# Moving the scan's input from PSUM into the scan's own result tile in SBUF

## The chip, the cores and the metric

The kernel runs on one core of one Trainium2 chip. The metric is the device time of one execution in microseconds (us). All verdicts below compare fast runs of kernels on the same chip; the profiles that are compared can be of different chips. "Before" is the kernel without the change, "after" the kernel with it.

## The reference, cut to what matters

The program is a network of four layers. The change touches layer 0 alone, a selective scan over 4096 pixels for 4 images, 4 directions, 192 channels and 16 states:

```python
def step(h, inp):
    d_t, u_t, b_t, c_t = inp
    dA = jnp.exp(d_t[..., None] * A)
    h = dA * h + (d_t * u_t)[..., None] * b_t[:, :, None, :]
    y = jnp.einsum('bkdn,bkn->bkd', h, c_t)
    return (h, y)
```

The other layers (a deformable convolution with gathers, a Fourier layer, feed-forward layers, attention) run beside the scan on the same engines, image by image.

## The kernel before

The scan is cut into 1536 units of 128 partitions (8 channels x 16 states) by 1024 pixels. Five engines hand each unit on, and the emission loop keeps the stages some units apart:

```python
# Layer0.scan: the stages of iteration n, in order (cut)
(self.inflow, n + 1), (self.total, n - 3 if n % 2 else -1), (self.decay, n + 2),
(self.keep, n - 1), (self.recur, n), (self.weigh, n - 1)

def decay(self, u):                      # ACT: da = exp(A * delta), in SBUF (five tiles)
    ...
    self.net.nc.scalar.activation(u.da, u.da, AF.Exp, scale=self.al[:, a : a + 1])

def inflow(self, u):                     # PE: db = delta * u, spread to 128 partitions
    db = self.ps.tile([128, 2, CH], F32, name=f"db{u.key}", tag="db", bufs=2)   # PSUM
    ...                                  # two matmuls, one for each half

def recur(self, u):                      # VectorE
    nc = self.net.nc
    nc.vector.tensor_mul(u.db, u.db, u.bc[:, 0, :])                              # L741
    u.hh = self.sp.tile([128, T], F32, name=f"hh{u.key}", tag="hh", bufs=3)      # SBUF
    first = 0.0 if u.step == 0 else u.state[:, u.n : u.n + 1]
    nc.vector.tensor_tensor_scan(                                                # L744
        u.along(u.hh), u.along(u.da), u.along(u.db), first, ALU.mult, ALU.add
    )

def keep(self, u):                       # ACT: the last column of hh is the next state
    ...
def weigh(self, u):                      # GpSimd: hc = hh * C
    u.hc = self.sp.tile([128, T], F32, name=f"hc{u.key}", tag="hc", bufs=3)
    self.net.nc.gpsimd.tensor_mul(u.hc, u.hh, u.bc[:, 1, :])                     # L755
def total(self, u, v):                   # PE: sums hc over the states (L772)
    ...
```

In PSUM the kernel keeps two db tiles (2 x 512 columns each), three tiles of 512 columns for the other matmuls and one for the sums.

## Time and profile before

| | before |
|---|---|
| time, median of the runs beside the kernel after | 10,588.9 us (10,575.5 to 10,604.1) |
| profiled execution shown in the prediction | 10,460.6 us, granted clock 0.702 |
| profiled execution taken later (`e5_before_again`) | 10,584.6 us, granted clock 0.696 |

The first profile is of an execution that was 1.2% faster than the timed runs. The second one, of the unchanged kernel, is the better partner for the kernel after, and the comparisons below use it. Its busy time in the stretch of the scans and in the stretch after the last scan (columns: the stretch, its length, then PE, weight loads, VectorE (DVE), ACT, GpSimd (POOL) with their counts, TensorE's granted clock, the DMA engines' share, GB/s):

```profile
322.00:9012.00 8690.00, 5842.08 (x22116) 1795.46 (x22118) 7215.60 (x4567) 3794.76 (x5988) 5960.76 (x3199) 0.69 0.67 171
9012.00:10584.00 1572.00, 1125.13 (x6192) 640.71 (x6190) 397.17 (x367) 412.84 (x787) 446.13 (x376) 0.68 0.23 64
```

The units occupy 8690 us, 5.66 us a unit, with VectorE busy for 83% and GpSimd for 69% of that. Neither is full, so what counts is how the two interlock. Its VectorE and GpSimd groups that matter (output<-inputs, shape, count, then busy us and mean ns, then idle time before the group and what ended it):

```profile
L744 DVE TENSOR_TENSOR_SCAN hh<-da,st,db 128x1024 f32<-128x1024 f32 x1152 | 2703.7, 2347 | 170.4 <-ACT st L751 31.8 <-ACT da L725 7.5 <-POOL hc L755 2.7
L741 DVE TENSOR_TENSOR db<-db,bc 128x1024 f32<-128x1024 f32 x1536 | 1871.6, 1218 | 572.9 <-PE db L730 571.5 <-DMA da<-de 1.1
L744 DVE TENSOR_TENSOR_SCAN hh<-da,db 128x1024 f32<-128x1024 f32 x384 | 878.1, 2287 | 109.1 <-ACT st L751 34.8 <-ACT da L725 31.2 <-DVE db L741 1.9
```

```profile
L755 POOL TENSOR_TENSOR hc<-hh,bc 128x1024 f32<-128x1024 f32 x1536 | 3876.9, 2525 | 1935.5 <-DVE hh L744 990.8 <-PE py L772 775.7 <-issue 68.3
L1074 POOL DMA_INDIRECT g<-table,idx x1152 | 1435.5, 1246 | 518.1 <-issue 193.1 <-DVE s L1091 146.3 <-DVE d L1234 117.6
```

### The profile page before, as it was taken

What the parts mean: (1) busy time and instruction counts of PE and PEld (TensorE: products, weight loads), DVE (VectorE), ACT (ScalarE), POOL (GpSimd) and SP (SyncE); (2) the same over time, 40 slices, a digit from 0 to 9 for tenths busy, and PEclk for the clock granted to TensorE, in tenths of its full rate; (3) what the DMA queues carried; (4) which work ended last, traced back from release to release, by engine and by line L of the source; (5) the groups of instructions that cost most, each with busy time, mean ns of one, the idle gap of its engine ahead of it and who ended that gap; (6) DMA issues with size and microseconds to landing.
All of it is one profiled execution on the core that took longest, in us unless ns stands there. A gap on an engine that the chain in (4) does not pass through costs nothing. (4 is left out here: it accounts for less than half of the span.)

```text
span 10460.6 us, 85850 instructions
## 1 busy us (share of the span) xinstructions
PE 7119.7 (68%) x28728; PEld 2481.0 (24%) x28728; DVE 7640.0 (73%) x4993; ACT 4352.7 (42%) x6950; POOL 6456.3 (62%) x3603
## 2 busy tenths in 40 slices
PE   7565865976794555558876665678676646877686
PEld 2010200311120111113332221133322112453262
DVE  0788688587759999987878889788888897444211
ACT  4564655665454443223433433333343423313223
POOL 0675476377537888875557878655678885366301
PEclk9555855866696666667777766677677666886695
DMA  1666565566656677776677667776767676543110
GB/s 45 166 174 157 149 173 162 140 172 168 156 134 171 184 188 185 189 181 161 177 184 184 169 160 190 172 179 166 186 174 176 174 188 151 118 137 92 52 45 6
DMA packets 775576, 1605.19 MB, mean 153 GB/s; under 512 B 249305, under 2 KB 339477, under 8 KB 773022
## 3 DMA queue, kind: packets, MB, share of 16 engines
q10 hardware_dynamic: 300672, 985.79, 37.4%
q1 hardware_dynamic: 400734, 387.34, 13.8%
q0 software_dynamic: 73728, 226.57, 8.3%
q8 instruction: 228, 3.74, 0.2%
q14 instruction: 214, 1.75, 0.1%
HBM read 1343.08 MB, written 256.29 MB: 153 GB/s over the span
## 5 line engine op out<-in xcount | busy, mean ns | idle before, releaser
L755 POOL TENSOR_TENSOR hc<-hh,bc 128x1024 f32<-128x1024 f32 x1536 | 3885.8, 2531 | 1937.3 <-DVE hh L744 1003.6
L725 ACT ACTIVATE da<-da,w_al 128x1024 f32<-128x1024 f32 x1536 | 1762.6, 1149 | 3126.4 <-DMA da<-de 981.5
L730 PE MATMUL db<-du,rep 96*128 96x512 bf16 x3072 | 1293.0, 515 | 2324.6 <-DVE hh L744 2147.1
L744 DVE TENSOR_TENSOR_SCAN hh<-da,st,db 128x1024 f32<-128x1024 f32 x1152 | 2703.5, 2347 | 165.4 <-ACT st L751 28.3
L741 DVE TENSOR_TENSOR db<-db,bc 128x1024 f32<-128x1024 f32 x1536 | 1871.0, 1218 | 585.3 <-PE db L730 585.0
L1074 POOL DMA_INDIRECT g<-table,idx x1152 | 1449.7, 1258 | 417.2 <-issue 191.1
L772 PE MATMUL py<-hc,w_fold 128*32 128x512 f32 x6144 | 1303.4, 886 | 25.4 <-POOL hc L755 8.8
L730 PEld LDWEIGHTS <-rep 96*128 96x128 bf16 x3072 | 231.2, 108 | 3539.8 <-DVE hh L744 2935.0
L744 DVE TENSOR_TENSOR_SCAN hh<-da,db 128x1024 f32<-128x1024 f32 x384 | 878.0, 2286 | 104.9 <-ACT st L751 31.5
L1085 DVE TENSOR_TENSOR g<-g,wt 128x3456 f32<-128x3456 f32 x128 | 593.1, 4634 | 148.6 <-DMA g<-table,idx 147.3
L605 POOL TENSOR_TENSOR w<-w,ex 128x512 f32<-128x512 f32 x192 | 259.0, 1349 | 650.7 <-ACT w L601 648.9
L518 PE MATMUL pc<-pad,wc 96*128 96x512 f32 x1152 | 533.1, 615 | 9.1 <-DMA wc<-wc_d 6.1
L607 DVE TENSOR_TENSOR rl<-rl,w 128x512 f32<-128x512 f32 x192 | 304.9, 1588 | 95.6 <-POOL w L605 95.3
L1102 PE MATMUL ps<-w_ident,s 128*96 128x128 f32 x1152 | 265.3, 378 | 136.9 <-DVE s L1091 120.7
L1332 POOL CAST xqf<-fl 96x512 fp8e5<-96x512 f32 x64 | 51.5, 810 | 496.6 <-DVE fl L1291 496.5
L604 DVE SCALAR_TENSOR_TENSOR rl<-pd,lw 128x512 f32<-128x512 f32 x192 | 130.7, 681 | 309.6 <-ACT lw L599 309.5
L592 PE MATMUL pd<-xd,dtw 7*128 7x512 f32 (+1 forms) x512 | 324.5, 953 | 43.9 <-ACT xd L570 28.5
L1103 ACT COPY st<-ps 96x384 f32<-96x384 f32 x384 | 177.5, 474 | 419.7 <-PE ps L1102 418.2
L772 PEld LDWEIGHTS py<-hc,w_fold 128*32 128x32 f32 x6144 | 184.8, 134 | 666.0 <-issue 516.2
L1109 PE MATMUL pd<-st,wdc 96*96 96x256 f32 x1152 | 309.0, 414 | 0.0
L518 PEld LDWEIGHTS pc<-pad,wc 96*128 96x128 f32 x1152 | 220.5, 195 | 310.5 <-issue 290.4
L628 DVE TENSOR_TENSOR du<-ex,du 128x512 bf16<-128x512 f32 x192 | 234.6, 1222 | 79.7 <-ACT du L626 75.3
(241 smaller groups left out, 10039.6 us busy)
## 6 DMA issues: line engine op xcount, KB each, us to landing
da<-de ACTq DMA_DIRECT2D x1536, 512.0 KB
du<-du ACTq DMA_DIRECT2D x384, 192.0 KB
bc<-bcd ACTq DMA_DIRECT2D x128, 512.0 KB
du<-du SPq DMA_DIRECT2D x128, 384.0 KB
y<-yb SPq DMA_DIRECT2D x384, 128.0 KB
de<-rl SPq DMA_DIRECT2D x128, 256.0 KB
m<-in_dft SPq DMA_DIRECT2D x128, 256.0 KB
du<-du SPq DMA_DIRECT2D x128, 192.0 KB
```

Of the source, the lines that this page charges most:

```text
L518: nc.tensor.matmul(pp, lhsT=wc[:, q, g * 128 : (g + 1) * 128], rhs=pad[:, r0 + dy : r0 + dy + NR, dx : dx + W], start=(q == 0), stop=(q == 8),
L592: nc.tensor.matmul(o, lhsT=dtw[2 * NS :, 2 * pr + q, m], rhs=xdbl[pr, j, q][2 * NS :], start=True, stop=True)
L607: nc.vector.tensor_sub(rl, rl, w1)
L725: self.net.nc.scalar.activation(u.da, u.da, AF.Exp, scale=self.al[:, a : a + 1])
L730: self.net.nc.tensor.matmul(db[:, h, :], lhsT=self.rep[:96, u.s % 4, :], rhs=u.du[u.s // 4][:, h * CH : (h + 1) * CH], start=True, stop=True,)
L741: nc.vector.tensor_mul(u.db, u.db, u.bc[:, 0, :])
L744: nc.vector.tensor_tensor_scan(u.along(u.hh), u.along(u.da), u.along(u.db), first, ALU.mult, ALU.add)
L755: self.net.nc.gpsimd.tensor_mul(u.hc, u.hh, u.bc[:, 1, :])
L772: nc.tensor.matmul(py[p0 : p0 + 32], lhsT=self.fold[:, u.i, :], rhs=hc[:, h * CH : (h + 1) * CH], start=u.add is None and u.i == 0, stop=( ...
L1074: nc.gpsimd.indirect_dma_start(out=g[:, k, :], out_offset=None, in_=self.tables[b % 2], in_offset=bass.IndirectOffsetOnAxis(ap=idx[:, 9 * ...
L1085: nc.vector.tensor_mul(g4, g4, w4.unsqueeze(2).to_broadcast([128, 36, C]))
L1109: nc.tensor.matmul(po, lhsT=wdc[:, k, :], rhs=st[:, k, :], start=(k == 0), stop=(k == 8))
```

## The change

The intent is to give a db tile back to PE one scan earlier, as PE stands for more than 2100 us waiting for one. The product of delta u and B goes into hh, and the scan runs over hh in place:

```diff
     def recur(self, u):
         nc = self.net.nc
-        nc.vector.tensor_mul(u.db, u.db, u.bc[:, 0, :])
         u.hh = self.sp.tile([128, T], F32, name=f"hh{u.key}", tag="hh", bufs=3)
+        nc.vector.tensor_mul(u.hh, u.db, u.bc[:, 0, :])
         first = 0.0 if u.step == 0 else u.state[:, u.n : u.n + 1]
         nc.vector.tensor_tensor_scan(
-            u.along(u.hh), u.along(u.da), u.along(u.db), first, ALU.mult, ALU.add
+            u.along(u.hh), u.along(u.da), u.along(u.hh), first, ALU.mult, ALU.add
         )
```

## The prediction

> **What bounds the kernel now.** I read the page first, then the busy time by stage, then the groups of instructions, then the list of who waited for whom, then a few microseconds of the timeline. The page says that no engine is full: VectorE (DVE) is busy for 73% of the span, PE 68%, GpSimd (POOL) 62%. The groups that the change touches, each line giving output<-inputs, shape, count, then busy us and mean ns, then idle time before the group and its releasers:
>
> ```profile
> L755 POOL TENSOR_TENSOR hc<-hh,bc 128x1024 f32<-128x1024 f32 x1536 | 3885.8, 2531 | 1937.3 <-DVE hh L744 1003.6 <-PE py L772 780.0 <-issue 65.6
> L744 DVE TENSOR_TENSOR_SCAN hh<-da,st,db 128x1024 f32<-128x1024 f32 x1152 | 2703.5, 2347 | 165.4 <-ACT st L751 28.3 <-ACT da L725 7.0 <-DVE db L741 1.5
> L741 DVE TENSOR_TENSOR db<-db,bc 128x1024 f32<-128x1024 f32 x1536 | 1871.0, 1218 | 585.3 <-PE db L730 585.0
> L1074 POOL DMA_INDIRECT g<-table,idx x1152 | 1449.7, 1258 | 417.2 <-issue 191.1 <-DVE d L1234 117.6 <-DVE s L1091 42.7
> L744 DVE TENSOR_TENSOR_SCAN hh<-da,db 128x1024 f32<-128x1024 f32 x384 | 878.0, 2286 | 104.9 <-ACT st L751 31.5 <-ACT da L725 30.6 <-DVE db L741 1.4
> ...
> L1085 DVE TENSOR_TENSOR g<-g,wt 128x3456 f32<-128x3456 f32 x128 | 593.1, 4634 | 148.6 <-DMA g<-table,idx 147.3 <-issue 1.2
> ```
>
> One unit of the scan is: PE spreads delta u into a PSUM tile db, VectorE multiplies it by B (L741) and scans it (L744), GpSimd multiplies the result by C (L755), PE sums that. There are 1536 units. The first scan starts at 323 us and the last ends at 8999 us: 8676 us, 5.65 us a unit. The busy time of that stretch:
>
> ```profile
> 323.00:8999.00 8676.00, 5834.19 (x22116) 1796.32 (x22118) 7201.01 (x4567) 3794.64 (x5989) 5955.84 (x3199) 0.69 0.67 171
> ```
>
> The columns are PE, weight loads, DVE, ACT, POOL: DVE 83%, POOL 69%. So VectorE leads, with GpSimd working beside it. From the waits, the one the change is aimed at:
>
> ```profile
> PE db L730 <- DVE hh L744: 2147.1, 730, 20.4
> ...
> DVE db L741 <- PE db L730: 585.0, 179, 22.0
> ```
>
> PE[...] stands 2147 us until a scan gives a db tile back (there are two); VectorE in turn stands 585 us for the next db.
>
> The 1461 us outside the stretch hold none of these units, and I take them as unchanged.
>
> [...] Two stretches of the timeline (start us, duration us):
>
> ```profile
> 4016.10 2.29 DVE L744 TENSOR_TENSOR_SCAN hh<-da,db 128x1024 f32<-128x1024 f32 x1
> 4017.03 2.36 POOL L755 TENSOR_TENSOR hc<-hh,bc 128x1024 f32<-128x1024 f32 x1
> ```
>
> ```profile
> 4024.81 2.35 POOL L755 TENSOR_TENSOR hc<-hh,bc 128x1024 f32<-128x1024 f32 x1
> ...
> 4025.16 3.66 DVE L607 TENSOR_TENSOR rl<-rl,w 128x512 f32<-128x512 f32 x1
> ...
> 4027.11 1.16 POOL L624 TENSOR_TENSOR ex<-ex,du 128x512 f32<-128x512 f32 x1
> ```
>
> The scan, with one input in PSUM, takes its shortest 2.29 us with GpSimd's product over it. L607, with both inputs in SBUF, takes 0.67 us when GpSimd is idle; here it takes 3.66 us and ends 0.55 us after GpSimd's second instruction: it waited through both. Over all 1536 scans with the state operand or without, the durations lie within 2.285 to 2.362 us, whatever GpSimd does.
> [...] L604 (one PSUM input, 128x512) has a mean of 0.681 us, L607 undisturbed 0.665 to 0.694. [...]
> [...]
>
> **The change part by part.** The order of instructions on each engine is the same in both kernels (compared). Nothing is added or removed; two operands move.
> - L741 writes hh in SBUF in place of db in PSUM. It still has one SBUF input, so 1536 x 1.22 us stay as they are and stay free beside GpSimd. hh is taken one instruction sooner; with three buffers it was last read three units earlier. Cost 0.
> - db is free after the product, one scan (2.33 us) sooner. Most of the 2147 us of PE's standing and of VectorE's 585 us can go. PE is not the leading engine, so the gain is at most those 585 us.
> - The scan now reads da and hh, both in SBUF. [...] 3582 us of scans no longer run beside GpSimd. Taking both engines' records together, GpSimd's tensor instructions lie over scans for 1930 us today, its gathers (L1074) for another 460 us. That parallel time is lost.
>
> The work that must now take turns, within the stretch, at undisturbed durations: scans 3582; L755 1536 x 2.35 = 3610; GpSimd's small products L605, L624, L610 and L616 (192 x 1.26, 192 x 1.15, 192 x 1.27) = 707 and L835 and L879 (128 x 1.25) = 160; VectorE's other instructions with two SBUF inputs L607 and L628 (384 x 0.68) = 261, and the 96 sampling tiles of the stretch (864 gathers, nine a tile) x (3.745 + 1.945 + 1.04 for L1085, L1088, L1091) = 646. Sum 8966 us, already over the 8676 us that the stretch takes. Gathers come on top: 864 x 0.96 = 829. Behind a two-input VectorE instruction they are held (about 4.3 us over L1085 against 0.96 otherwise), but one that has started does not hold VectorE back (L628 over such a gather stays at 0.69). I count half: 8966 + 415 = 9380 us.
>
> No queue of turns is filled without gaps: from a scan's end to the product that it releases I see 0.13 to 0.15 us at best[...]. VectorE reaches 83% today; with two engines feeding one turn I choose 92%: 9380 / 0.92 = 10,200 us, **1520 us more**. A second way: 8676 + 1930 + half of 460 - 585 = 10,250 us, 1575 us more. I take 1510, on the median of 10,589 us: **12,100 us**.
>
> **Rivals.** *The early release wins.* For it: the 2147 and 585 us. It would give about 10,000 to 10,400 us. Against: it holds only if scans don't exclude GpSimd, and every two-input instruction in this trace does. *The exclusion hides in the slack.* For it: VectorE idles 17% of the stretch, GpSimd 31%, and the waits that the release ends become room; then the stretch comes near 8970, about 10,900 us. Against: in the stages with gathers GpSimd is already 80 to 88% busy (438 of 500 us from 4000 to 4500), and about a quarter of the units follow each other at 3.60 us or less today, where scan and product in turn need about 4.65. *Full serialization*: all gathers count and the turn is 88% used: 9795 / 0.88 = 11,130, about 13,000 us, if GpSimd's back-to-back instructions keep VectorE out as they did at 4025 us.
>
> **Range and chances.** The first rival has perhaps 4%, a result within 2% another 5%. The low end, 11,300, is the second rival with some gaps; the high end, 12,900, almost the third.
>
> **What would show it.** The scan's mean should rise from 2.33 us to 3 to 3.6, its minimum stay at 2.25 to 2.35, with long ones ending just after a GpSimd instruction; L755's mean should rise over 2.53; the product (line 742 after the change) should stay at 1.22. PE's wait for VectorE's release of db should fall under 600 us, VectorE's wait for db under 200. The stages with gathers should stretch most; the time after the last scan should stay near 1460 us. I am wrong if the scans keep their 2.29 to 2.36 us (no exclusion: then the first rival), or if they lengthen but the stretch doesn't (slack).

8966 + 415 = 9380 us, over 0.92 that is 10,200 us, 1520 us more than the 8676 of the stretch, and the forecast is 10,589 + 1510 = 12,100 us. What carries it:

- That the scan with two SBUF inputs will take turns with GpSimd is inference from other instructions of the trace before. Of the L607 that start with more than 0.2 us of a GpSimd tensor instruction still to run, 138 of 139 run over 0.1 us beyond their shortest time (0.665 us), as do 48 of 55 L1085 (shortest 3.731); in the eight others GpSimd's product itself took 3.4 to 6.3 us against its median of 2.36.
- That the move itself would not shorten the scan was an assumption, and no saving was counted either; the comparison of L604 (0.681 us) with L607 (0.665 to 0.694) in the text belongs to it. The result bears it out: the shortest scan is 2.291 us, against 2.285 before.
- That an engine which waits lets no later instruction past can't be read from one trace. As measured, VectorE's 4993 records and GpSimd's 3603 come in the same order in the traces before and after. The 92% is a choice.

## The result, and the profile after

The kernel after takes 11,813.0 us (median of 4 runs, 11,812.8 to 11,822.8) against 10,588.9 us: 1224 us more. The ratio is 1.1158 (95% interval 1.1138 to 1.1177). Ratios here are the mean time of one kernel's fast runs over that of the other's fast runs of the same rounds, so they are not quite the ratios of the medians that are quoted.

The busy time of the kernel after in its scans' stretch and after its last scan:

```profile
322.00:10243.00 9921.00, 6395.97 (x22119) 1948.73 (x22118) 8942.17 (x4567) 3804.04 (x5989) 7491.07 (x3199) 0.67 0.59 150
10243.00:11811.00 1568.00, 1116.22 (x6188) 642.74 (x6188) 398.25 (x367) 412.20 (x786) 453.16 (x376) 0.69 0.23 64
```

All of the added time lies in the stretch of the scans (8690 to 9921 us, 1231 more); the end is unchanged (1572 and 1568 us). VectorE and GpSimd run the same instructions (their counts are equal), but VectorE's busy time grew by 1727 us and GpSimd's by 1530 us. The groups show where:

```profile
L755 POOL TENSOR_TENSOR hc<-hh,bc 128x1024 f32<-128x1024 f32 x1536 | 4083.1, 2659 | 1855.2 <-DVE hh L744 1244.0 <-PE py L772 485.4 <-PE db L730 15.8
L744 DVE TENSOR_TENSOR_SCAN hh<-da,st,hh 128x1024 f32<-128x1024 f32 x1152 | 3921.3, 3404 | 63.6 <-ACT da L725 5.2 <-DVE hh L742 1.4
L1074 POOL DMA_INDIRECT g<-table,idx x1152 | 2312.5, 2007 | 503.5 <-issue 232.0 <-DVE s L1091 129.7 <-DVE d L1234 117.7
L742 DVE TENSOR_TENSOR hh<-db,bc 128x1024 f32<-128x1024 f32 x1536 | 1854.1, 1207 | 500.1 <-PE db L730 359.3 <-POOL hc L755 98.8 <-ACT st L751 36.8
...
L744 DVE TENSOR_TENSOR_SCAN hh<-da,hh 128x1024 f32<-128x1024 f32 x384 | 1304.8, 3398 | 22.3 <-ACT da L725 6.6
```

The product (L742) is as short as ever, 1.21 us, and so is the shortest scan (2.291 us). But the mean scan went from 2.33 to 3.40 us, and the gather (L1074) from 1.25 to 2.01 us. The timeline of VectorE, then of GpSimd, over one stretch shows what happens inside (start us, duration us):

```profile
5020.38 1.19 DVE L742 TENSOR_TENSOR hh<-db,bc 128x1024 f32<-128x1024 f32 x1
5021.61 4.18 DVE L744 TENSOR_TENSOR_SCAN hh<-da,hh 128x1024 f32<-128x1024 f32 x1
```

```profile
5021.27 2.36 POOL L755 TENSOR_TENSOR hc<-hh,bc 128x1024 f32<-128x1024 f32 x1
5023.79 2.79 POOL L1074 DMA_INDIRECT g<-table,idx  x1 [0.16 <-issue]
5026.89 0.95 POOL L1074 DMA_INDIRECT g<-table,idx  x1 [0.30 <-issue]
```

The scan is issued at 5021.61, while GpSimd's product runs (to 5023.63). It ends at 5025.79, which is 2.16 us after the product: it stood until GpSimd had finished, then ran. The gather issued at 5023.79 meets the running scan and takes 2.79 us, to 5026.58, that is 0.79 us past the scan's end; the next gather, with no scan over it, takes 0.95. Of the 1536 scans of this profile, 1054 start under a product; 93% of these end 2.05 to 2.2 us after it does. All 185 that start with GpSimd idle take their shortest time. Each engine's wait is booked as its busy time: the scan's record is 4.18 us long where its shortest is 2.29, the gather's 2.79 where the next takes 0.95. A long busy bar is therefore no proof of work: here 1.89 and 1.84 us of the two are waiting.

The waits that the change was aimed at, PE's in the second profile of before, then both in the kernel after:

```profile
PE db L730 <- DVE hh L744: 2124.2, 708, 20.1
```

```profile
PE db L730 <- DVE hh L742: 1885.4, 596, 15.1
...
DVE hh L742 <- PE db L730: 359.3, 115, 14.2
```

PE is now let go by the product in place of the scan, and still stands 1885 us (2124 before). VectorE's wait for db went from 572 to 359 us.

### The profile page after: what moved, and what is told of

It reads as the page before. It is cut to its first block, busy times and chain, and to the rows that moved or that the text cites. A ratio compares the mean times of both kernels' runs of the same rounds, so it can differ in the third digit from the quotient of the medians.

```text
span 11811.1 us, 85922 instructions
## 1 busy us (share of the span) xinstructions
PE 7741.5 (66%) x28728; PEld 2666.9 (23%) x28728; DVE 9381.7 (79%) x4993; ACT 4361.7 (37%) x6950; POOL 7970.7 (67%) x3603
## 5 line engine op out<-in xcount | busy, mean ns | idle before, releaser
L755 POOL TENSOR_TENSOR hc<-hh,bc 128x1024 f32<-128x1024 f32 x1536 | 4083.1, 2659 | 1855.2 <-DVE hh L744 1244.0
L744 DVE TENSOR_TENSOR_SCAN hh<-da,st,hh 128x1024 f32<-128x1024 f32 x1152 | 3921.3, 3404 | 63.6 <-ACT da L725 5.2
L1074 POOL DMA_INDIRECT g<-table,idx x1152 | 2312.5, 2007 | 503.5 <-issue 232.0
L742 DVE TENSOR_TENSOR hh<-db,bc 128x1024 f32<-128x1024 f32 x1536 | 1854.1, 1207 | 500.1 <-PE db L730 359.3
L772 PE MATMUL py<-hc,w_fold 128*32 128x512 f32 x6144 | 1707.9, 916 | 685.6 <-POOL hc L755 659.4
L744 DVE TENSOR_TENSOR_SCAN hh<-da,hh 128x1024 f32<-128x1024 f32 x384 | 1304.8, 3398 | 22.3 <-ACT da L725 6.6
L730 PEld LDWEIGHTS <-rep 96*128 96x128 bf16 x3072 | 295.5, 111 | 3124.1 <-issue 2848.8
L605 POOL TENSOR_TENSOR w<-w,ex 128x512 f32<-128x512 f32 x192 | 302.4, 1575 | 496.6 <-ACT w L601 496.4
L1085 DVE TENSOR_TENSOR g<-g,wt 128x3456 f32<-128x3456 f32 x128 | 562.2, 4392 | 80.8 <-DMA g<-table,idx 75.0
L518 PE MATMUL pc<-pad,wc 96*128 96x512 f32 x1152 | 532.1, 614 | 10.7 <-DMA wc<-wc_d 7.7
L607 DVE TENSOR_TENSOR rl<-rl,w 128x512 f32<-128x512 f32 x192 | 327.7, 1707 | 94.4 <-POOL w L605 92.5
L624 POOL TENSOR_TENSOR ex<-ex,du 128x512 f32<-128x512 f32 x192 | 377.6, 1967 | 31.8 <-ACT du L622 30.0
L1109 PE MATMUL pd<-st,wdc 96*96 96x256 f32 x1152 | 393.1, 499 | 8.0 <-issue 4.2
L628 DVE TENSOR_TENSOR du<-ex,du 128x512 bf16<-128x512 f32 x192 | 324.0, 1688 | 52.8 <-ACT du L626 38.2
L604 DVE SCALAR_TENSOR_TENSOR rl<-pd,lw 128x512 f32<-128x512 f32 x192 | 129.9, 677 | 241.1 <-ACT lw L599 241.1
```

Of the source, the lines that this page charges most:

```text
L518: nc.tensor.matmul(pp, lhsT=wc[:, q, g * 128 : (g + 1) * 128], rhs=pad[:, r0 + dy : r0 + dy + NR, dx : dx + W], start=(q == 0), stop=(q == 8),
L624: nc.gpsimd.tensor_sub(ex, ex, du[:, 0, :])
L730: self.net.nc.tensor.matmul(db[:, h, :], lhsT=self.rep[:96, u.s % 4, :], rhs=u.du[u.s // 4][:, h * CH : (h + 1) * CH], start=True, stop=True,)
L742: nc.vector.tensor_mul(u.hh, u.db, u.bc[:, 0, :])
L744: nc.vector.tensor_tensor_scan(u.along(u.hh), u.along(u.da), u.along(u.hh), first, ALU.mult, ALU.add)
L772: nc.tensor.matmul(py[p0 : p0 + 32], lhsT=self.fold[:, u.i, :], rhs=hc[:, h * CH : (h + 1) * CH], start=u.add is None and u.i == 0, stop=( ...
```

## The experiments

**Theory:** the scan's second SBUF input makes it take turns with every GpSimd instruction that reads SBUF. **Rival:** the move itself costs, through the earlier hold on hh, another order in which PE is released, or a lower clock. A second question is what the early release of db is worth by itself.

### GpSimd's product replaced by a fill

Both kernels, with GpSimd's big product turned into a fill that reads nothing. The result is wrong.

```diff
-        self.net.nc.gpsimd.tensor_mul(u.hc, u.hh, u.bc[:, 1, :])
+        self.net.nc.gpsimd.memset(u.hc, 0.0)
```

> Kernel before, with GpSimd's product (hc = hh x C) replaced by a fill of hc with zeros; wrong result on purpose. A reference for e2. GpSimd then reads no SBUF in 1536 of its instructions. Both theories: faster than the 10,589 us of before, 9,800 to 10,500 us, scans unchanged at 2.29 to 2.36 us.

> Kernel after, with the same fill in place of GpSimd's product. Exclusion theory (a scan with two SBUF inputs and a GpSimd instruction that reads SBUF take turns): with the reads of L755 gone only the small products (867 us) are left to exclude, so the ratio to e1 is 0.96 to 1.03, the scan's mean under 2.7 us. Rival (the move itself costs: the earlier hold on hh, the order in which PE is let go, the clock): the ratio to e1 stays at 1.08 to 1.12.

Measured: 10,137.6 us for the kernel before with the fill and 10,241.2 us for the kernel after with it. Their ratios to the same runs of before are 0.9583 and 0.9674, so after over before is 1.0095. The change costs 0.95% instead of 11.6%. The scans of the kernel after with the fill (all instructions of one line, durations ns as minimum/median/maximum):

```profile
L744 DVE TENSOR_TENSOR_SCAN hh<-da,st,hh x1152: 2349/2351/4280, 445.5 to 8660.0; 128x1024 f32<-128x1024 f32 x192
L744 DVE TENSOR_TENSOR_SCAN hh<-da,hh x384: 2290/2292/4280, 323.2 to 8263.8; 128x1024 f32<-128x1024 f32 x192
```

The median scan is back at its shortest length (2.351 us, shortest 2.349), although its inputs lie in SBUF and GpSimd's 1536 fills (0.96 us each) still write SBUF. The long ones left (221 over 2.4 us) lie over GpSimd's small products and casts. The rival would have kept the 8 to 12%. One part of it is not tested here: the fill doesn't read hh, so GpSimd's hold on hh is gone as well. That part is settled by the experiment with da in PSUM below, where GpSimd's product still reads hh.

### Almost nothing on GpSimd that reads SBUF

To see the move with almost nothing left to exclude, the GpSimd tensor products, sums and differences of the scan's stretch were made fills, and the gathers became plain loads on the sync queue (results wrong, and equally wrong: relative error 0.3205 in both). The expectation says that every GpSimd read is gone; in fact some 90 casts and copies of the stretch were left.

```diff
-        nc.gpsimd.tensor_sub(w1, w1, ex)
+        nc.gpsimd.memset(w1, 0.0)
...                                      # likewise L610, L616, L624, L755, L835, L879
-                    nc.gpsimd.indirect_dma_start(out=g[:, k, :], ..., in_=self.tables[b % 2], ...)
+                    nc.sync.dma_start(g[:, k, :], self.tables[b % 2][128 * t : 128 * t + 128, :])
```

> Kernel before, wrong on purpose: every GpSimd instruction of the scan's stretch that reads SBUF is replaced by a fill with zeros (L605, L610, L616, L624, L755, L835, L879) and the gathers by plain loads of the same size on the sync queue. Reference for e8; VectorE's instructions with two SBUF inputs keep their shortest times. 9,700 to 10,300 us.

> Kernel after with the same edits as e7. With nothing left to exclude, what remains is the move by itself with its early release of db. Exclusion theory, early release worthless: ratio to e7 0.985 to 1.01, and e2's 1.0% is gone. Early release worth what the prediction allowed (585 us): 0.93 to 0.96. Rival (the move itself disturbs): 1.03 or more. Scans at 2.29 to 2.36 us in all cases.

Measured: 9956.3 and 9862.0 us, ratios 0.9421 and 0.9335, so after over before is 0.991: the move by itself gains at most 94 us. (The two profiled executions are 105 us apart, and 30 of these lie after the last scan, at a granted clock of 0.72 and 0.74.) The scans of the kernel after:

```profile
L740 DVE TENSOR_TENSOR_SCAN hh<-da,st,hh 128x1024 f32<-128x1024 f32 x1152 | 2716.7, 2358 | 65.9 <-ACT da L721 8.1 <-DVE hh L738 1.4
```

Nine of them are longer than 2.4 us (up to 3.62), and all nine lie over one of the casts that were left. VectorE's wait for db, before and then after:

```profile
DVE db L737 <- PE db L726: 608.7, 189, 20.5
```

```profile
DVE hh L738 <- PE db L726: 605.1, 168, 19.3
```

It did not change. So those 600 us are not the price of a db tile held through the scan: PE is late for reasons of its own, and a tile that is free earlier doesn't make it come earlier. The trace of the kernel after shows what PE does in these 605 us: it runs convolution and Fourier matmuls outside the scan (L518 for 201 us, L971 for 122, L1176 for 71), and the spread itself for 138. The early release is worth at most about 1% here, not the 585 us that the prediction allowed at most. This was measured with GpSimd relieved of its reads; in the kernel after itself it can't be taken apart.

### The scan with one SBUF input again, the product still in SBUF

The second SBUF input can be avoided the other way round: keep the product in hh in place and the early release, and let ACT write da into PSUM. There da takes the place of db's second tile, so db keeps one, and with one tile each the stages have to be emitted in another order. The control keeps that order and the single db tile but leaves da in SBUF.

```diff
-        self.net.nc.scalar.activation(u.da, u.da, AF.Exp, scale=self.al[:, a : a + 1])
+        dp = self.ps.tile([128, 2, CH], F32, name=f"dp{u.key}", tag="dp", bufs=1)
+        dp = dp.rearrange("p h t -> p (h t)")
+        self.net.nc.scalar.activation(dp, u.da, AF.Exp, scale=self.al[:, a : a + 1])
+        u.da = dp
...                                      # both kernels: db bufs=1, and the order
-   inflow n+1, total n-3, decay n+2, keep n-1, recur n, weigh n-1
+   total n-3, keep n-1, recur n, inflow n+1, decay n+1, weigh n-1
```

> Kernel after, with the decay factor da written by ACT's exponential into PSUM (one tile of two banks, taken from db, which keeps one tile), so that the scan has one SBUF input again while the product stays in hh in place and db is still let go after the product; the stages are emitted in another order, since one tile each forces exp and spread of unit n+1 behind the scan and product of n. Exclusion theory: scans back at 2.25 to 2.36 us, total 10,200 to 11,000 us. Rival: 11,500 us or more.

> Kernel after with the stage order and the single db tile of e3_da_in_psum, but with da left in SBUF: it differs from e3 only in where the exponential writes. Exclusion theory: scans at a mean of 3.2 to 3.6 us and a total of 11,700 to 12,500 us, so that e3's 10,957 us is 800 us or more below it. If the new order [...] made e3 faster than after: about 10,950 us here too.

Measured: 10,956.7 us with da in PSUM (ratio to before 1.0354) and 12,037.5 us with da in SBUF (1.1388). The two differ only in where the exponential writes, and that is worth 0.1034 of before, some 1090 us. In both the scan runs in place and GpSimd's product holds hh, so neither the hold nor the scan in place is the cause. The scans with da in PSUM, first, and in SBUF:

```profile
L746 DVE TENSOR_TENSOR_SCAN hh<-dp,st,hh 128x1024 f32<-128x1024 f32 x1152 | 2706.8, 2350 | 379.3 <-ACT dp L726 279.1 <-DVE hh L744 3.3 <-issue 0.4
```

```profile
L743 DVE TENSOR_TENSOR_SCAN hh<-da,st,hh 128x1024 f32<-128x1024 f32 x1152 | 3712.8, 3223 | 273.4 <-ACT da L724 169.0 <-DVE hh L741 2.3 <-ACT yb L781 0.5
```

With one input in PSUM, whichever of the two, the scan keeps its time: 2.350 us with da there, 2.347 with db. It is no better kernel than before: with a single tile for da, ACT's exponential stands 3146 us waiting for scans to end, and VectorE waits 381 us for it (279 us before the scans shown and 102 before the 384 others). The new order with its single db tile costs 2.1% by itself (1.1388 over 1.1158).

### The change in every second unit

```diff
+        pr = u.hh if u.s < 4 else u.db
-        nc.vector.tensor_mul(u.hh, u.db, u.bc[:, 0, :])
+        nc.vector.tensor_mul(pr, u.db, u.bc[:, 0, :])
...                                      # and the scan reads pr
```

> Kernel after in every second unit (768 scans with both inputs in SBUF), kernel before in the others. Exclusion theory: the units in PSUM keep scans of 2.29 to 2.36 us, the others are near 3.4; about half of the 1224 us that the whole change cost: 11,200 us (11,000 to 11,400). Rival (a disturbance of the order): no particular split of the scan times, and not half.

Measured: 11,047.3 us, 474 us over the before of these runs, ratio 1.0444. The scans of the two kinds in one execution:

```profile
L745 DVE TENSOR_TENSOR_SCAN hh<-da,st,hh 128x1024 f32<-128x1024 f32 x576 | 1908.1, 3313 | 33.9 <-ACT da L725 4.8 <-DVE hh L743 0.5
L745 DVE TENSOR_TENSOR_SCAN hh<-da,st,db 128x1024 f32<-128x1024 f32 x576 | 1351.8, 2347 | 71.0 <-ACT st L752 3.9 <-ACT da L725 1.0 <-DVE db L743 0.9
```

Neighbouring scans, with the same engines and buffers around them and in the same execution (granted clock 0.696), take 3.31 us when both inputs are in SBUF and 2.35 when one is in PSUM. Half of the units cost 39% of the whole (474 of 1224 us), a little under half: the fewer the turns, the more of them fit into idle time. That last clause is my reading; no run tests it alone.

### A second profile of the kernel before

> Kernel before, unchanged, for a second profile: the first profiled execution took 10,463 us while its timed runs take 10,575 to 10,614, and the stretch after the last scan took 1462 us there but 1556 to 1582 us in every other kernel so far. If that was a more generous clock in one execution, this profile has 10,560 to 10,610 us and about 1560 us after the last scan, and the change adds nothing there. If the change lengthens the end, it stays near 1462 us.

Measured: 10,586.7 us (a single run, so its state is unknown). The stretch after the last scan, shown in the table of before above, has 1572 us at a granted clock of 0.68; the first profile had 1461 us at 0.73 there. Length times clock is nearly the same, 1069 and 1067. So the change leaves the end alone, and some 110 us of the apparent difference between the first profile and that of the kernel after go with the clock of one execution.

### The gathers taken off GpSimd

Both kernels with the plain loads of the experiment without reads, and nothing else (sampling is wrong).

```diff
-                    nc.gpsimd.indirect_dma_start(out=g[:, k, :], ..., in_=self.tables[b % 2], ...)
+                    nc.sync.dma_start(g[:, k, :], self.tables[b % 2][128 * t : 128 * t + 128, :])
```

> Kernel before with the 1152 gathers replaced by plain loads of the same size on the sync queue (other rows, so sampling is wrong on purpose): GpSimd's queue loses 1450 us of records. Reference for e10. 10,200 to 10,650 us.

> Kernel after with the same plain loads. The prediction put half of the gathers' 829 us into the turn. If that is right, the cost of the change falls from about 1240 us by about 440 us (415 / 0.945): 700 to 900 us over e9, ratio 1.065 to 1.09. If gathers run wholly in the shadow of the scans: 1050 us or more over e9 (ratio 1.10 or more). If all of them are in the turn: 300 to 450 us (ratio 1.03 to 1.045).

Measured: 10,291.4 and 11,272.5 us, 981 us apart, after over before 1.0957. None of my three bands holds that. I had taken the saving from the kernel after alone, but the kernel before gains too: in units of the common before (10,503 us), the plain loads save 0.0202 of it in the kernel before (212 us) and 0.0422 in the kernel after (1.1158 less 1.0736, 443 us). The 443 us look like what half of the gathers in the turn would give (440 by the working above), but they aren't all from the turn. After the last scan, where there is no turn, this profile has 1418 us at a clock of 0.74, against 1568 at 0.69. The stretch of the scans is 9517 us against 9921, 404 less, or some 320 less when one allows for this chip, on which before itself is 0.8% faster (10,503 against 10,589 us). At 94.5% that is 300 to 380 of the gathers' 829 us, an estimate: somewhat under half. The plain loads also change which queue the loads stand in, so this is agreement and not proof.

## Why the prediction was right, point by point

The verdict and the size were right: slower, 1224 us where 1510 were predicted, and 11,813 us lies inside 11,300 to 12,900. The 1510 stands below both of the prediction's sums, 1520 and 1575, without a reason given. By its steps:

- **The scan excludes GpSimd: right, and shown.** The mean scan of 3.40 us lies in the 3 to 3.6 that were named, its minimum of 2.29 us is the old one, L755 rose to 2.66 us, the product stayed at 1.21. Taking GpSimd's reads away takes the cost away (1.0095 and 0.991 left), and an input in PSUM takes the long scans away. One sign was told wrongly: the long scans don't end "just after a GpSimd instruction" but about 2.15 us after it, since they wait first and run then.
- **What must take turns, 9380 us: right as far as it can be checked.** The scan's stretch came to 9921 us, not 10,200. 9380 over 9921 is 94.5%; without the gathers, 8966 over 9517 is 94.2% (93.5% with the 0.8% of that run's chip). The two agree within a point, so the term that was mis-sized is the choice "two engines feeding one turn I choose 92%": it measured 94%. With 94.5% in place of 92% the prediction's stretch is 9926 us and not 10,196. That accounts for 270 of the 287 us by which the prediction was too high. The split between gathers and filling rests on this agreement.
- **"hh is taken one instruction sooner ... Cost 0": wrong by a little.** The product now waits 98.8 us for GpSimd to release hh (the groups above), where the scan waited for it 2.7 us before.
- **The second way to the sum: near the result by luck of its parts.** It gave back 585 us for the early release. The experiment without reads gives at most 94 us for it. But 1930 + 230 us of lost overlap less 1231 us measured leaves 929 us that were given back, of which the release explains a tenth. Of the rest the profiles show this: VectorE's busy time grew by 1727 us and not by 2160, and 496 us of that went into its idle time in the stretch (1474 to 979 us).
- **"PE's wait for VectorE's release of db should fall under 600 us, VectorE's wait for db under 200": wrong.** They are 1885 and 359 us. The release does come one scan sooner within a unit, but VectorE comes later with every unit, and PE is back at the next db tile and waits for the product. So the wait moved to the next event: 1885 of the 2124 us are still there.
- **The stages with gathers stretch most: right, mildly.** The time of each 192 units, from the records of the second profile of before and of the profile after, with the gathers that fall into it:

| units | before us | after us | added | gathers | mean scan after us |
|---|---|---|---|---|---|
| 0 to 191 | 1104 | 1247 | 143 | 0 | 3.15 |
| 192 to 383 | 1269 | 1406 | 137 | 0 | 3.14 |
| 384 to 575 | 1189 | 1375 | 186 | 103 | 3.65 |
| 576 to 767 | 1065 | 1253 | 187 | 185 | 3.58 |
| 768 to 959 | 960 | 1089 | 129 | 94 | 3.35 |
| 960 to 1151 | 1074 | 1233 | 158 | 194 | 3.52 |
| 1152 to 1343 | 962 | 1086 | 124 | 94 | 3.32 |
| 1344 to 1535 | 1065 | 1230 | 166 | 194 | 3.50 |

  Groups with 185 gathers or more stretch by 15 to 18%, those with none by 11 to 13%. With the gathers replaced by plain loads, the six groups that had gathers stretch by 9 to 14% and the first two by 14 and 11%, nearly as above, so the extra goes with the gathers.
- **The time after the last scan stays: right** (1572 and 1568 us), once both are read at a like clock.

Two things stay open. A fourth hh tile, to take away the 99 us that the product now waits for GpSimd to release hh, could not be tried (the program doesn't build with it, so there is no run), so that share of the cost was read from the trace and not tested. And why the two-engine turn fills to 94% and not to some other share is not explained, only measured.

## What to carry to other kernels

Before moving a VectorE operand from PSUM to SBUF, count the SBUF inputs of the instruction that reads it. Here the scan with two of them stopped running beside the GpSimd products that read SBUF: its mean went from 2.33 to 3.40 us, while beside GpSimd's fills it was 2.43, and the waits stand in the busy time of both engines (1727 us more on VectorE, 1530 on GpSimd). The evidence was in the profile before the change, in another instruction with two SBUF inputs that shows a mean over its minimum (L607: 1.588 us against 0.665). And ask whether a buffer's late release is what makes the next producer late; the long wait of an engine with slack doesn't show that. Here PE stood 2124 us for db, and the earlier release gained at most 94 us.

## What else the traces show of the two engines

- The scan is among the instructions that take turns with GpSimd: 3.31 us with two SBUF inputs beside 2.35 with one, in the same execution.
- A gather behaves otherwise than GpSimd's products. A product holds VectorE back to its end, and a second one right behind it does so too (in the trace before, L607 took 3.66 us through both, against 0.67 alone). A gather that has started does not (L628 over one stays at 0.69 us; of the 100 scans of the kernel after that start over a gather, 85 take their shortest time). But a gather issued under a scan or a `tensor_tensor` with two SBUF inputs stands past its end (by 0.80 us in the median under the scans of the kernel after; it takes 2.79 us under a scan, a mean of 4.1 to 4.2 under L1085, against 0.95).
- Where the scan's input lies doesn't show in its shortest time: 2.291 us with both inputs in SBUF and 2.285 with one in PSUM.
